# Two Mamba layers with states of eight channels on the partitions instead of one state of 128 channels at a time

## The chip, the cores and the metric

The kernel runs on one core of one Trainium2 chip. The metric is device time in microseconds of one execution of the whole program. The engines named here are PE (TensorE, the matrix array), DVE (VectorE), ACT (ScalarE), POOL (GpSimd) and SP (which issues most of the transfers). Each has a queue of instructions that it takes in order; they meet at semaphores. SBUF is the on-chip memory of 128 partitions, PSUM the smaller memory that PE writes to, in 8 banks of 512 f32 per partition.

## What is computed

The reference is a network of four layers on an image batch `x` of shape (4, 56, 56, 128), all in f32. Layer 0 is a windowed attention, layer 1 a pair of Mamba blocks, layer 2 an additive attention and an expert layer, layer 3 an attention and a mixture of experts. Each result is added to `x`. Only layer 1 and the group norm in front of layers 0 and 1 are touched. Cut to what matters, layer 1 is:

```python
h = gn(x).reshape(b * n, t, d)            # 4*56 sequences of 56 steps, d = 128
for l in range(2):
    u, res = split(h @ in_w[l])           # 256 inner channels each
    u = silu(causal_depthwise_conv(u, conv_w[l], 4 taps) + conv_b[l])
    dt, Bm, Cm = split(u @ x_proj_w[l], [8, 24])    # 8 + 16 + 16
    delta = softplus(dt @ dt_proj_w[l] + dt_proj_b[l])
    A = -exp(A_log[l])                    # (256, 16)
    # per sequence, for each channel d and each state n, s starts at 0:
    #   s[t,d,n] = exp(delta[t,d] * A[d,n]) * s[t-1,d,n] + delta[t,d] * u[t,d] * Bm[t,n]
    #   y[t,d]   = sum_n s[t,d,n] * Cm[t,n]
    h = ((y + u * D[l]) * silu(res)) @ out_proj_w[l]
x = x + h
```

There are 256 x 16 = 4096 independent recurrences over time for each sequence.

## The kernel before

Everything stays on the chip between the layers. `X[b]` holds image b as 28 tiles of 112 tokens (two image rows each). Layer 1 works on chunks of CH = 448 tokens, which are SEQ = 8 whole sequences of HW = 56 steps. There are NCH = 7 chunks an image, 4 images and 2 Mamba blocks, so 56 pairs of a chunk and a block; I call one such pair a step. For an image the order is chunks 0 to 3 of block 0, the same of block 1, then chunks 4 to 6 likewise (`order` in `layer1`).

For a step the 256 inner channels lie on the partitions in NHALF = 2 halves of 128, time along the free dimension. `mamba_pre` prepares a step: the input projection on PE, the copy into a padded tile `up` (L480), the causal convolution as one `tensor_scalar` and three `scalar_tensor_tensor` per half on DVE (L483, L488), Silu on ACT, the projection `dbl` to dt, B and C (L500), delta with a softplus built from Abs, Exp and Ln on ACT and four operations on POOL (L515 to L523), and du = delta * u on DVE (L525).

`mamba_scan` then loops over the DS = 16 states. For state n, PE broadcasts the row of B and the row of C to all partitions by a matmul with a column of the identity (L541), ACT makes dA = exp(A * delta) with A as a scale per partition (L549), DVE makes dBu = B * du (L553), runs the recurrence over 2 x 448 elements as one scan (L555), and multiplies by C (L559); PE adds the product into y with an identity matmul (L561). The decay tiles `dA` have a zero at the first step of every sequence, so that one scan restarts at each. In the middle of the loop (n = 8) `midway` issues the preparation of the next step. At the end DVE forms yg = (u * D + y) * silu(res) (L566, L569) and PE projects it.

The tile framework decides the order in each engine's queue when the program is built, from the program's order and its own estimates, and gives buffers from pools of a fixed number (`bufs`). So a line of the loop can stand in a queue a little before or behind its place in the text, but not past what its pool allows. All loads of a layer's weights are issued by SP at the layer's start, when the previous layer's memory is free.

`group_norm` transposes an image by PE into PSUM, copies it (alternately DVE and ACT), takes statistics of the copy on DVE (L143), combines them over groups of four channels by a small matmul, and normalises in place (L161). It is called once per image in layer 0 and in layer 1.

Of the kernel before, what the change touches and what calls it, by code (L numbers as in the profile page):

```python
# [35 lines left out]
DBL = DR + 2 * DS  # L36

# [16 lines left out]
def host_constants():  # L54
# [7 lines left out]
    for d in range(KR):  # L62
# [5 lines left out]
    place[p, QW - JG + p // AH] = 1.0  # L68
    return {
        "k_toep": toep.reshape(1 + KR, HW * HW),  # L70
# [6 lines left out]
class Hybrid:  # L77
# [57 lines left out]
    def group_norm(self, b, pool, psum, tag, group):  # L135

        nc = self.nc
        xn = self.t(pool, [P, S], "xnT")
        st = self.t(pool, [P, NCH, nc.vector.BN_STATS_DIM], "gn_st")
        for c in range(NCH):  # L140
            ch = xn[:, c * CH : (c + 1) * CH]
            self.transposed_chunk(psum, tag, self.X[b], c, ch)
            nc.vector.bn_stats(st[:, c, :], ch)  # L143
# [15 lines left out]
        for c in range(NCH):  # L159
            ch = xn[:, c * CH : (c + 1) * CH]  # L160
            nc.vector.tensor_scalar(ch, ch, mean, r, op0=ALU.subtract, op1=ALU.mult)  # L161
# [122 lines left out]
    def layer0(self):  # L284
        nc, a, tc = self.nc, self.a, self.tc
        with ExitStack() as ctx:
# [24 lines left out]
            for b in range(B):  # L311
                xn = self.group_norm(b, big, ps_m, "m", group)
# [74 lines left out]

    def layer1(self):
        nc, a, tc = self.nc, self.a, self.tc
        with ExitStack() as ctx:  # L390
            wp = ctx.enter_context(tc.tile_pool(name="l1_w", bufs=1))
            w = {}
            group = self.load(wp, [P, P], "group1", a["k_group"])
            w["in"] = self.load(
                wp, [P, NL, 2 * DI], "in_w", a["L1_conv_in_proj_w"].rearrange("l p f -> p l f")
            )
            by_channel = lambda n, r: a[n].rearrange(r, p=P)
            w["xw"] = self.load(
                wp, [P, NL, NHALF, DBL], "xw", by_channel("L1_conv_x_proj_w", "l (h p) k -> p l h k")
            )  # L400
            w["dtw"] = self.load(
                wp, [DR, NL, DI], "dtw", a["L1_conv_dt_proj_w"].rearrange("l r d -> r l d")
            )
            w["ow"] = self.load(
                wp, [P, NL, NHALF, C], "ow", by_channel("L1_conv_out_proj_w", "l (h p) m -> p l h m")
            )
            w["A"] = self.load(
                wp, [P, NL, NHALF, DS], "A", by_channel("L1_conv_A_log", "l (h p) n -> p l h n")
            )
            nc.scalar.activation(w["A"], w["A"], AF.Exp)  # L410
            nc.vector.tensor_scalar(w["A"], w["A"], -1.0, None, op0=ALU.mult)
            w["cw"] = self.load(
                wp, [P, NL, NHALF, DC], "cw", by_channel("L1_conv_conv_w", "l (h p) o k -> p l h (o k)")
            )
            with nc.allow_non_contiguous_dma(reason="vectors, by partition"):
                for k, n in (("cb", "conv_b"), ("dtb", "dt_proj_b"), ("D", "D_param")):
                    w[k] = self.load(
                        wp, [P, NL, NHALF], k, by_channel("L1_conv_" + n, "l (h p) -> p l h")
                    )

            w["dA"] = []
            for i in range(3):
                dA = self.t(wp, [P, NHALF, SEQ, HW], f"dA{i}")
                nc.vector.memset(dA, 0.0)
                w["dA"].append(dA)
            self.n_dA = 0

# [3 lines left out]
            ps_b = ctx.enter_context(tc.tile_pool(name="l1_b", bufs=2, space=PSUM))  # L431
            ps_y = ctx.enter_context(tc.tile_pool(name="l1_y", bufs=1, space=PSUM))
            for b in range(B):
                xn = self.group_norm(b, big, ps_m, "m", group)


                h = {c: xn[:, c * CH : (c + 1) * CH] for c in range(NCH)}
# [4 lines left out]
                for i, (c, l) in enumerate(order):  # L442
# [5 lines left out]
                    yg = self.mamba_scan(l, w, pre.pop((c, l)), sm, ps_b, ps_y, prepare_next)  # L448
                    if l < NL - 1:
                        po = self.t(ps_m, [P, 512], "m")  # L450
                        for f in range(NHALF):
                            nc.tensor.matmul(
                                po[:, :CH], w["ow"][:, l, f, :], yg[:, f],
                                start=(f == 0), stop=(f == NHALF - 1),
                            )
                        h[c] = self.t(sm, [P, CH], "h", bufs=5)
                        nc.scalar.copy(h[c], po[:, :CH])
                        continue
# [10 lines left out]
    def mamba_pre(self, l, h, w, sm, ps_m):  # L469

        nc = self.nc
        seqs = lambda ap: ap.rearrange("p (s t) -> p s t", t=HW)
        us = self.t(sm, [P, NHALF, CH], "us")
        sres = self.t(sm, [P, NHALF, CH], "sres")
        for f in range(NHALF):
            ps = self.t(ps_m, [P, 512], "m")
# [4 lines left out]
            u = us[:, f]  # L481
            cw = w["cw"][:, l, f, :]
            nc.vector.tensor_scalar(  # L483
                seqs(u), up[:, :, DC - 1 :], cw[:, DC - 1 : DC], w["cb"][:, l, f : f + 1],
# [488 lines left out]
```

## Time and profile before

| what | value |
|---|---|
| median of 3 runs | 11,997.65 us (11,997.62 to 12,001.13) |
| profiled execution | 12,008.86 us, span 12,007.1 us |
| mean granted clock of PE | 0.896 |
| PE busy | 10,754.4 us, 90% |
| DVE busy | 5,358.3 us, 45% |
| ACT busy | 6,301.1 us, 52% |
| POOL busy | 668.6 us, 6% |

The profile describes one execution. A group line names the kernel line, the engine, the operation, the tiles and shapes and the count, then after the bar the busy time of the group in us and the mean duration of one in ns, then the idle time of the engine just before these instructions and what ended it. An f32 matmul appears as two records. The matmuls' ends are modelled, so the start-to-start time says more than the duration. The granted clock is the share of full speed that PE was given; a window line gives it for a stretch. A line of a stretch gives the window, its length, and for each engine the busy time and the number of instructions.

The layers follow one another in time: layer 0 to about 1045 us, layer 1 to about 5750, the additive attention to about 8900, the rest to the end. In the row of 40 slices each slice is 300 us.

### The profile page before, as it was taken

The page shows a single profiled execution, that of the slowest core. Times are in us where ns is not written, and L with a number is a line of the kernel's source. Part 1 is how long each engine was busy: PE and PEld are TensorE (multiplying, and loading weights), DVE is VectorE, ACT ScalarE, POOL GpSimd, SP SyncE. Part 2 cuts the span into 40 slices and gives each one's busy share as a digit, 9 for nine tenths or more (in the row PEclk, how much of TensorE's full clock was granted, in tenths as well). Part 3 has the DMA queues.
Part 4 walks back from the last instruction along what each step waited for, and adds up shares of the span by engine and source line. Part 5 has one row for each costly group of instructions (what it writes and reads, how often), then busy time and mean ns, then how long its engine had stood idle before and what let it go on. Part 6 is the DMA issues. An engine that isn't in the chain of part 4 may idle for free.

```text
span 12007.1 us, 105563 instructions
## 1 busy us (share of the span) xinstructions
PE 10754.4 (90%) x41247; PEld 4699.9 (39%) x41247; DVE 5358.3 (45%) x7960; ACT 6301.1 (52%) x10749; POOL 668.6 (6%) x494
## 2 busy tenths in 40 slices
PE   7888888888988888888899999999999979998988
PEld 3443333333333333333333333333333358655655
DVE  3446898888988888888300000000000031123033
ACT  2223443334434343443799899899899911322322
POOL 0000111111111111111000000000000000000000
PEclk8887888888888888888999999999999956999999
DMA  1000000000000000000000000000000012000000
GB/s 36 1 1 4 0 0 0 0 0 0 0 0 0 0 0 0 0 0 0 1 1 1 1 1 1 1 1 1 1 1 1 1 50 65 1 6 6 1 6 6
DMA packets 90323, 59.06 MB, mean 5 GB/s; under 512 B 21012, under 2 KB 81244, under 8 KB 89756
## 3 DMA queue, kind: packets, MB, share of 16 engines
q1 hardware_dynamic: 89821, 52.30, 1.6%
q8 instruction: 324, 5.31, 0.2%
q14 instruction: 178, 1.45, 0.0%
HBM read 45.21 MB, written 7.07 MB: 4 GB/s over the span
## 4 chain that ended last, share of the span: by engine, by line
PE 67%; DVE 16%; issue 7%; ACT 6%; POOL 4%; SPq 0%; DMA 0%; ACTq 0%; POOLq 0%; DVEq 0%
PE s L651 24%; PE y L561 8%; PE o L851 7%; PE s L844 5%; DVE hs L555 4%; PE o L660 4%; PE C L541 3%; DVE hs L559 3%; PE B L541 2%; ACT e L656 2%; DVE dBu L553 2%; PE d L369 2%; PE o L369 2%; DVE us L488 2%; POOL sp_e L521 1%
## 5 line engine op out<-in xcount | busy, mean ns | idle before, releaser
L646 ACT ACTIVATE th<-fT,g 128x448 f32<-128x448 f32 (+3 forms) x6272 | 3328.9, 622 | 17.5 <-DVE g L627 17.5
L651 PE MATMUL s<-th,place 128*32 128x448 f32 (+4 forms) x12544 | 3183.1, 515 | 7.0 <-ACT th L646 7.0
L549 ACT ACTIVATE dA<-delta,A 128x440 f32<-128x440 f32 x1792 | 1092.8, 654 | 2296.7 <-DVE hs L555 2289.3
L671 DVE TENSOR_SCALAR den<-o 112x1 f32<-112x1 f32 x224 | 31.8, 152 | 4961.7 <-PE o L660 3644.1
L561 PE MATMUL y<-hs,ident 128*128 128x448 f32 x3584 | 1795.7, 639 | 427.6 <-DVE hs L559 424.1
L555 DVE TENSOR_TENSOR_SCAN hs<-dA,dBu 128x896 f32<-128x896 f32 x896 | 1797.2, 2024 | 0.6
L651 PEld LDWEIGHTS s<-th,place 128*32 128x32 f32 (+1 forms) x12544 | 786.7, 106 | 2131.9 <-ACT th L646 2032.5
L561 PEld LDWEIGHTS y<-hs,ident 128*128 128x128 f32 x3584 | 730.3, 220 | 1474.0 <-DVE hs L559 814.2
L541 PE MATMUL B<-dbl,ident 40*128 40x448 f32 x1792 | 900.4, 607 | 186.0 <-DVE dBu L553 185.5
L559 DVE TENSOR_TENSOR hs<-C,hs 128x896 f32<-128x896 f32 x896 | 947.4, 1077 | 49.5 <-PE C L541 48.2
L849 ACT ACTIVATE e<-s,shift 112x448 f32<-112x448 f32 x784 | 496.3, 634 | 886.4 <-PE s L844 839.0
L553 DVE TENSOR_TENSOR dBu<-B,du 128x896 f32<-128x896 f32 x896 | 943.0, 1074 | 0.0
L541 PE MATMUL C<-dbl,ident 40*128 40x448 f32 x1792 | 880.3, 593 | 0.0
L851 PEld LDWEIGHTS o<-xa,e 112*112 112x112 f32 x6272 | 711.1, 176 | 297.5 <-ACT e L849 295.6
L851 PE MATMUL o<-xa,e 112*112 112x129 f32 x6272 | 789.3, 279 | 13.5 <-ACT e L849 0.9
L844 PE MATMUL s<-xT 128*112 128x448 f32 x1568 | 654.6, 539 | 0.0
L541 PEld LDWEIGHTS B<-dbl,ident 40*128 40x128 f32 x1792 | 340.5, 202 | 648.1 <-DVE dBu L553 341.6
L660 PE MATMUL o<-xa,e 112*112 112x129 f32 x3248 | 492.3, 288 | 106.2 <-ACT e L656 98.5
L660 PEld LDWEIGHTS o<-xa,e 112*112 112x112 f32 x3248 | 384.5, 176 | 447.2 <-ACT e L656 402.5
L357 ACT ACTIVATE e<-s 112x896 f32<-112x896 f32 (+1 forms) x272 | 206.4, 801 | 602.0 <-PE s L352 434.9
L541 PEld LDWEIGHTS C<-dbl,ident 40*128 40x128 f32 x1792 | 299.6, 192 | 536.9 <-issue 491.8
L361 DVE TENSOR_TENSOR e<-e,e_inner 112x560 f32<-112x560 f32 (+5 forms) x416 | 238.2, 612 | 358.5 <-ACT e L357 357.3
(218 smaller groups left out, 7666.3 us busy)
## 6 DMA issues: line engine op xcount, KB each, us to landing
w<-in_L_ffn_weight SPq DMA_DIRECT2D x16, 1024.0 KB
w<-in_L_ffn_weight SPq DMA_DIRECT2D x64, 256.0 KB
X<-in_x SPq DMA_DIRECT2D x8, 784.0 KB
out<-X SPq DMA_DIRECT2D x8, 784.0 KB
e_edge<-dtab SPq DMA_DIRECT2D x42, 49.0 KB
e_inner<-dtab SPq DMA_DIRECT2D x14, 49.0 KB
dtab<-tab SPq DMA_DIRECT2D x1, 637.0 KB
in_w<-in_L_conv_in_proj_w SPq DMA_DIRECT2D x1, 512.0 KB
```

What stands on the lines that cost most here:

```text
L541: nc.tensor.matmul(ps[:, :CH], self.ident[0:DBL, at : at + 1].to_broadcast([DBL, P]), dbl, start=True, stop=True,)
L549: nc.scalar.activation(dA[:, f, :, 1:], seqs(delta[:, f])[:, :, 1:], AF.Exp, scale=w["A"][:, l, f, n : n + 1])
L553: nc.vector.tensor_mul(dBu, bc[0], du)
L555: nc.vector.tensor_tensor_scan(hs.rearrange("p f c -> p (f c)"), dA.rearrange("p f s t -> p (f s t)"), dBu.rearrange("p f c -> p (f c)"), ...
L559: nc.vector.tensor_mul(hs, bc[1], hs)
L561: nc.tensor.matmul(py[f][:, :CH], self.ident, hs[:, f], start=(n == 0), stop=(n == DS - 1))
L646: nc.scalar.activation(th[:, lo:], fT[:, c * CH + lo : (c + 1) * CH], AF.Tanh, bias=g[:, at : at + 1])
L651: nc.tensor.matmul(ps[QW * blk : QW * blk + rows, lo:CH], place[:, off : off + rows], th[:, lo:], start=(q == 0), stop=(n + 1 == NG or q = ...
L660: nc.tensor.matmul(po[s][:TP, : C + 1], e[:, s * TP : (s + 1) * TP], xa[:, J, :], start=(J == 0), stop=(J == TC * c + s),)
L844: nc.tensor.matmul(ps[:TP, :CH], xT[:, t * TP : (t + 1) * TP], xT[:, c * CH : (c + 1) * CH], start=True, stop=True,)
L849: nc.scalar.activation(e, ps[:TP, :CH], AF.Exp, bias=shift)
L851: nc.tensor.matmul(po[s][:TP, : C + 1], e[:, s * TP : (s + 1) * TP], xa[:, t, :], start=(t == 0), stop=(t == NT - 1),)
```

## The change

Layer 1 is rearranged so that 8 channels x 16 states lie on the 128 partitions.

- The loop over 16 states becomes a loop over 32 groups of eight channels, taken in pairs: 16 iterations a step, each with two groups `k` that sit in different quarters of 32 partitions. Per group, PE expands delta of 8 channels to 128 partitions with the factor -A folded into the selection matrix (`A`, L606: 32 rows by 128 columns, so that the two groups' matmuls use different row tiles of the array), ACT takes Exp of both groups in place in PSUM (L609), PE expands du likewise (`u`, L613), DVE multiplies it with B (L617) and scans 448 elements with the decay read from PSUM (L618).
- The product with C moves to POOL, one instruction over both groups (L621).
- The sum over the 16 states is a matmul with a 0/1 matrix of 128 x 32 (`sum`, L623), into 32 partitions of y, so that the two groups use different column tiles. u * D enters y as a matmul with a diagonal matrix (L597), and the gating is one product per half (L627).
- B and C come replicated from a matmul with a weight of 128 columns (L556), two per chunk and half.
- The convolution is folded into the input projection: four weights, one per tap, and four accumulating matmuls over shifted views of h (L539), so h and the normalised x carry three zeros before each sequence. The bias enters at the Silu.
- delta comes straight from u by a weight that is the product of the two small projections (L567), formed once. The restart of the scans comes from setting delta to 1e30 at each sequence's first step (L586), so that the decay is exp(-large) = 0. du is made on POOL (L582).
- The weights that this needs are formed once on DVE and PE in `layer1_weights`.
- `group_norm` takes its statistics from PSUM, not from the copy, and can leave room for the zeros.

The core of the diff:

```diff
-        nc.vector.tensor_mul(du, delta, us)
-        return us, sres, dbl, delta, du
+        nc.gpsimd.tensor_mul(du, delta, us)
+        first = delta.rearrange("p f (s t) -> p f s t", t=HW)[:, :, :, 0:1]
+        for f in range(NHALF):
+            nc.gpsimd.memset(first[:, f], LONG)
+        return us, sres, bc, delta, du
...
-        py = [self.t(ps_y, [P, 512], f"y{f}") for f in range(NHALF)]
-        for n in range(DS):
-            if n == DS // 2:
-                midway()
-            bc = []
-            for tag, at in (("B", DR + n), ("C", DR + DS + n)):
-                ps = self.t(ps_b, [P, 512], tag)
-                nc.tensor.matmul(
-                    ps[:, :CH], self.ident[0:DBL, at : at + 1].to_broadcast([DBL, P]), dbl,
-                    start=True, stop=True,
-                )
...
-            for f in range(NHALF):
-                nc.scalar.activation(
-                    dA[:, f, :, 1:], seqs(delta[:, f])[:, :, 1:], AF.Exp, scale=w["A"][:, l, f, n : n + 1]
-                )
-            nc.vector.tensor_mul(dBu, bc[0], du)
-            nc.vector.tensor_tensor_scan(
...
-            nc.vector.tensor_mul(hs, bc[1], hs)
...
         for f in range(NHALF):
+            py = self.t(ps_m, [P, 512], "m")
+            nc.tensor.matmul(py[:, :CH], w["Dd"][:, l, f, :], us[:, f], start=True, stop=False)
+            for r0 in range(0, P // HD, 2):
+                for q in range(QG):
+                    if (f, r0, q) == (0, 2, 2):
+                        midway()
+                    pa = self.t(ps_a, [P, 2, 512], "a")
+                    hs = self.t(sm, [P, 2, CH], "hs", bufs=3)
+                    for k in range(2):
+                        own = rows(r0 + k)
+                        nc.tensor.matmul(
+                            pa[:, k, :CH], w["A"][own, l, f, q, :], delta[own, f], start=True, stop=True
+                        )
+                    nc.scalar.activation(pa[:, :, :CH], pa[:, :, :CH], AF.Exp)
+                    for k in range(2):
+                        own = rows(r0 + k)
+                        pu = self.t(ps_u, [P, 512], "u")
+                        nc.tensor.matmul(
+                            pu[:, :CH], w["pick"][own, q, :], du[own, f], start=True, stop=True
+                        )
+                        dBu = self.t(sm, [P, CH], "dBu", bufs=3)
+                        nc.vector.tensor_mul(dBu, pu[:, :CH], bc[:, 0])
+                        nc.vector.tensor_tensor_scan(
+                            hs[:, k], pa[:, k, :CH], dBu, 0.0, op0=ALU.mult, op1=ALU.add
+                        )
+                    nc.gpsimd.tensor_mul(hs, hs, bc[:, 1:2].to_broadcast([P, 2, CH]))
+                    for k in range(2):
+                        nc.tensor.matmul(
+                            py[rows(r0 + k), :CH], w["sum"][:, q, :], hs[:, k],
+                            start=False, stop=(q == QG - 1),
+                        )
+            nc.vector.tensor_mul(yg[:, f], py[:, :CH], sres[:, f])
```

In `mamba_pre` the convolution and the small projections:

```diff
-            nc.tensor.matmul(ps[:, :CH], w["in"][:, l, f * P : (f + 1) * P], h, start=True, stop=True)
-            up = self.t(sm, [P, SEQ, HW + DC - 1], f"up{f}")
-            nc.gpsimd.memset(up[:, :, 0 : DC - 1], 0.0)
-            nc.scalar.copy(up[:, :, DC - 1 :], seqs(ps[:, :CH]))
...
+            for k in range(DC):
+                nc.tensor.matmul(
+                    seqs(ps[:, :CH]), w["in"][:, l, k, own], h[:, :, k : k + HW],
+                    start=(k == 0), stop=(k == DC - 1),
+                )
+            nc.scalar.activation(us[:, f], ps[:, :CH], AF.Silu, bias=w["cb"][:, l, f : f + 1])
...
+        for i in range(2):
+            ps = self.t(ps_m, [P, 512], "m")
+            for f in range(NHALF):
+                nc.tensor.matmul(
+                    ps[:, :CH], w["bc"][:, l, i, f, :], us[:, f], start=(f == 0), stop=(f == NHALF - 1)
+                )
+            nc.scalar.copy(bc[:, i], ps[:, :CH])
...
+            for g in range(NHALF):
+                nc.tensor.matmul(
+                    ps[:, :CH], w["dt"][:, l, g, f * P : (f + 1) * P], us[:, g],
+                    start=(g == 0), stop=(g == NHALF - 1),
+                )
```

The pools of layer 1 in PSUM are `ps_m` (2 banks: y, and every product of the preparation), `ps_a` (2 x 2 banks) and `ps_u` (2 banks); before, they were `ps_m` (2), `ps_b` (2 each for B and C) and `ps_y` (2).

More of the change, by code (lines that the diff above doesn't have):

```diff
@@ L159, in group_norm @@
         for c in range(NCH):
[L160 to L161 removed]
+            nc.vector.tensor_scalar(chunk(c), chunk(c), mean, r, op0=ALU.subtract, op1=ALU.mult)
         return xn
@@ L391, in layer1 @@
             wp = ctx.enter_context(tc.tile_pool(name="l1_w", bufs=1))
[L392 to L395, printed above, removed]
-            )
-            by_channel = lambda n, r: a[n].rearrange(r, p=P)
-            w["xw"] = self.load(
-                wp, [P, NL, NHALF, DBL], "xw", by_channel("L1_conv_x_proj_w", "l (h p) k -> p l h k")
-            )
[L401 to L426, printed above, removed]
+            w = self.layer1_weights(wp)
             big = ctx.enter_context(tc.tile_pool(name="l1_big", bufs=2))
```

168 lines of the change are left out of this document (110 added, 58 removed).

## Prediction

> **What bounds the kernel now.** I read the page first (busy times, slices, costliest groups), then stretches of the second stage, then groups by shape. From the page:
> ```profile
> PE 10754.4 (90%) x41247; PEld 4699.9 (39%) x41247; DVE 5358.3 (45%) x7960; ACT 6301.1 (52%) x10749; POOL 668.6 (6%) x494
> DVE  3446898888988888888300000000000031123033
> PEclk8887888888888888888999999999999956999999
> L555 DVE TENSOR_TENSOR_SCAN hs<-dA,dBu 128x896 f32<-128x896 f32 x896 | 1797.2, 2024 | 0.6
> L553 DVE TENSOR_TENSOR dBu<-B,du 128x896 f32<-128x896 f32 x896 | 943.0, 1074 | 0.0
> L559 DVE TENSOR_TENSOR hs<-C,hs 128x896 f32<-128x896 f32 x896 | 947.4, 1077 | 49.5 <-PE C L541 48.2
> ```
> The shares mix stages. The changed stage is where the DVE digits are 8 and 9, 1093 to 5748 us; scan and products there (L553, L555) have next to no idle time before them: VectorE is the bound. One step (one chunk, one layer; 56 in all) runs from one gating (L566) to the next, 2514.45 to 2595.80. Busy times of PE, PEld, DVE, ACT, POOL, then the granted clock:
> ```profile
> 100.00:1040.00 940.00, 801.59 (x5488) 377.71 (x5485) 417.79 (x668) 233.56 (x317) 25.88 (x21) 0.80 0.00 1
> 2514.45:2595.80 81.35, 71.60 (x153) 26.83 (x152) 73.37 (x63) 32.91 (x49) 11.25 (x6) 0.90 0.00 0
> 449.18:452.59 3.41, 2.06 (x26) 1.24 (x26) 1.31 (x3) 1.88 (x3) 0.00 (x0) 1.00 0.00 0
> 452.59:456.00 3.41, 3.41 (x27) 1.62 (x24) 1.10 (x3) 0.00 (x0) 0.00 (x0) 0.50 0.02 5
> ```
> A step is 81.35 us, DVE 73.37 of it; 56 x 81.35 = 4556 of the stage's 4655. Rows 3 and 4 show the clock: a stretch in which PE was busy 2.06 of 3.41 us is followed by one at half clock. The other prices, from groups by shape and matmuls in order of time:
> ```profile
> L357 ACT ACTIVATE e<-s 112x896 f32<-112x896 f32 x224 | 196.4, 915 | 526.1 <-PE s L352 434.9 <-issue 84.9 <-ACT e L357 6.3
> L377 DVE TENSOR_TENSOR oT<-o,r 128x448 f32<-128x448 f32 x28 | 17.2, 613 | 0.1
> L523 POOL TENSOR_TENSOR delta<-delta,sp_ln 128x896 f32<-128x896 f32 x56 | 116.9, 2087 | 4.4
> 601.34 0.73 PE L352 MATMUL s<-qT,kT 32*112 32x280 f32 x4 [0.98 <-ACT e L357]
> 2586.25 1.01 PE L541 MATMUL C<-dbl,ident 40*128 40x448 f32 x2
> 2587.10 0.91 PE L541 MATMUL B<-dbl,ident 40*128 40x448 f32 x2
> 2587.95 1.77 PE L561 MATMUL y<-hs,ident 128*128 128x448 f32 x4
> ```
> An f32 matmul leaves two records; start to start, one of 448 columns takes 0.85 us (C to B to y). L352's four records are two matmuls in different row tiles, done in the time of one, so a pair of row tiles costs about 0.9, and so do two column tiles.
>
> **The change by engine, per step.** DVE loses 16 x (1.07 + 2.02 + 1.08) = 66.7, the convolution 2 x (0.50 + 3 x 0.68) = 5.1, du 1.09 and 1.2 of the gating. It gains 32 products at 0.61 (L377) and 32 scans, each half of L555 and a share of fixed cost, 1.08: 54.1. About 57 remain: 16 us less. PE has 3 pairs in each of 16 iterations (A, u, sum; about 41 us) and some 20 single matmuls for the next chunk (convolution 8, gate 2, B and C 4, delta 4, D 2; 16 us). POOL gains 16 products at 2.07 and du. The memsets it gains (two of 8 columns on delta, one on h; L479's 0.12 each) replace two of `up`. ACT's table loads (1.28) rise from 4.5 to 10, since four Silu now stand between Exp; its busy time is 16 x 0.92 + 7 + 13 = 35 in 105, and only the two loads counted below lie on the path. No engine is full in 81 us, so the order decides.
>
> **The order of the built program.** PE takes its queue in order. Sum(i) needs POOL's product of iteration i, which needs both scans of i. The queue repeats two forms: "A(i) u0(i) sum(i-1) u1(i)" in 7 of 16 iterations (split), else "A(i) u0 u1 sum(i-1)". Behind each sum stand A(i+1) and, when split, u1(i), so VectorE's next product waits for POOL, and the scan behind it too.
> Let E(i) be the end of the second scan. Split: POOL 2.07 + 0.07 handover, sum 0.85, u1 0.8, drain and handover 0.2, then product and scan 1.6: E(i) = E(i-1) + 5.6. An unsplit one after it is bound by DVE, 3.2. Unsplit behind unsplit: E(i+1) = E(i-1) + 2.14 + 0.85 + 0.9 + 0.75 + 0.2 + 3.2 = E(i-1) + 8.0, 4.0 each. The sequence is 13 to 15 unsplit, 0 and 1 split, 2 unsplit, 3 split, 4 unsplit, 5 split: 3.2 + 4.8 + 3.2 + 6.1 (with 0.5 of the gating product) + 5.6 + 3.2 + 5.6 + 3.2 + 5.6 = 40.5 for 9 iterations.
> The preparation falls into iterations 6 to 12:
> - 5 to 6: POOL 2.14, sum 0.85, A 0.9, u0 0.75, four convolution matmuls 3.0 in the queue before u1, u1 1.0, product and scan 1.6 = 10.2. 6 to 7: 5.6.
> - 7 to 12: POOL 2.14, sum 0.85, u1 0.75, half of A 0.75, eight matmuls (B, C, delta) 6.0, drain 0.2: 10.7. ACT: Abs 0.63, load 1.28, Exp 0.95, the iteration's Exp 0.95, load 1.28, Ln 0.95: 6.0. POOL: softplus add 2.07, add-subtract 3.2, product 9, three more (du with them), and only then product 10: 6 x 2.07 + 3.2 = 15.6. Then sum 0.85, A 0.9, u0 0.95, DVE 1.6, u1 and the rest 1.6: 5.9. Total 38.2.
> Together 54; the step is 54.0 + 40.5 = 94.5 at full clock, against 81.35. Before, the chain through POOL showed once a step, as 6.35 us of idle DVE ahead of du, because no product of the scan stood in POOL's queue; moving du to POOL removes that wait and its 1.09, and product 10 and sum(10) are late next.
> PE work on that path is 20 us in iterations 6 to 12 and 10 in the others. At half clock the step is 94.5 + 30 = 124.5. A pair of iterations keeps PE busy 5.7 of 8.8 us, about the share (2.06 of 3.41) after which the clock fell; at half clock PE is nearly always busy, after which it came back. The first stage, which alternates so (PE busy 0.85 of it), has a mean of 0.80, that is 0.4 of the time at half clock; I take that: 1 / (0.6/94.5 + 0.4/124.5) = 105 us a step. Its bounds are 94.5 (always full) and 124.5 (always half).
> The Trainium skill, "TensorE: Matmul & The Clock Gate", section "Why this matters for your kernels", asks for no PE-idle gaps over about 3 us to avoid a drop; by that the clock stays full here and the time would be 12,730 (an estimate); the row at 449 us shows a drop with 2.06 of 3.41 us busy, and I follow the row.
> "TensorEngine Tiling (Array Packing)", section "Key Properties", says that changing the tiling mode drains TensorE, which speaks against alternating row and column tiles; a drain of 0.16 us (a record's 0.54 less 0.38 of streaming) twice an iteration would be 5 us a step, some 290 in all (estimate); no row here has that switch without a wait, and the sum leaves it out.
>
> **Small parts.** Weights: 13 loads in place of 11 on SP (0.4 to 0.8 each to issue), a 1 MB broadcast, and some 30 DVE instructions at 0.2 to 0.6 stand before the first group norm's statistics or beside them, where three clears (2.7) stood: 0 to 20 once; I take 15, nearest to the DVE sum. Group norm reads statistics from PSUM: 0.61 (L377, PSUM) against 0.62, 56 times: nothing, at most 4 either way. The first preparation of a batch runs uncovered before and after (33 us before: 1060.7 to 1093.8); 5 to 10 more, four times. Against that, the last step of each batch has none to carry: 54 less 7 iterations at 4.3, that is 24, against some 13 (convolution, delta and du on DVE 7.6, the wait 6.35), four times. These cancel within 60, and I count them as nothing.
>
> **Sum.** 56 x (105 - 81.35) = +1324 on the profiled execution's 12,008.9 (span 12,007.1): 13,333. The median before, 11,997.65, stands 11 lower: 13,320.
> Prices that no row has: the scan of 448 with one input in PSUM is at least half of L555, 1.01, and at most 1.08 + 0.18 (a 448 tensor_scalar took 0.68 from PSUM, L516, and 0.50 from SBUF, L483); I take 1.08, nearest to L555; the upper end is 32 x 0.18 = 5.8 a step, 325 in all. Exp in place in PSUM over 2 x 448: L357 has 0.92 for the same shape read from PSUM, and two of L549 make 1.3; the path holds it once a step (iteration 9; elsewhere it ends 0.3 before the scan needs it), so 0.4 a step, 22 in all; I take 0.95. POOL's product with a broadcast factor: L523 has 2.07 for 896, and the add with a broadcast in the first stage 1.27 for 512, which is 2.2 for 896; the upper end adds 8 x 0.15, 67 in all.
>
> **Rivals.**
> - Full clock throughout: 94.5 a step, 12,008.9 + 56 x 13.15 - 11 = 12,730. For it: 2507 to 2547 us ran at 0.99; against it: PE was 96% busy there.
> - Row tiles not side by side, or half clock nearly always: pairs of A and u at 1.7 in place of 0.9, 14 a step on top of 105 (A on 16 paths at 0.8, u partly), or 124.5 straight: 13,320 + 784 = 14,100 to 14,410. L352's row is against the first, but with 112 columns, not 128.
> - Faster: POOL's product is much quicker than L523. POOL holds 8 x 2.14 + 15.6 = 33 of the 94.5; at full clock the break-even is a saving of 13.15, all of POOL at 0.6 of its rows, the product at about 1.25 us instead of 2.07. At 1.1 the step is 79 and the time 11,870; with POOL wholly out of the way (DVE 57 and the 8 that it idles now) 11,080. For it: POOL's busy spans are rough; against it: L520, L522 and L523 lie at 2.07 to 2.4, and a sum(i) released by DVE alone isn't in the program.
> - No change: 105 would have to fall to 81; nothing else does that.
>
> **How the numbers follow.** Chances: the forecast 0.52 (own range 12,950 to 13,800), full clock 0.22, the slow rival 0.17, faster 0.08, same 0.01. The range leaves out the faster case, the lower edge of the full-clock case and the upper of the slow one: 12,500 to 14,300. A difference under 0.2% can't be told from none here.
>
> **What would show it.** After: DVE busy near 57 us a step with its largest idle put down to PE u; PE's largest wait for POOL hs (L621 of the changed kernel); iterations of 3.2 and 5.6 in turn; a clock near 0.80 in this stage; one stall of some 15 us a step behind POOL's softplus. I am wrong if L621 is near 1.1 us, if the clock digits stay 9, or if the row tiles start 0.85 apart.

## The result, and the profile of the changed kernel

The changed kernel takes 14,229.17 us (median of 4 runs, 14,225.5 to 14,234.95), the kernel before 11,997.64 beside it: a ratio of 1.186, with a 95% interval of 1.184 to 1.188. The forecast was 13,320 with a range of 12,500 to 14,300. Sign and range hold, but the time lies 429 us above the top of the likeliest case's own range (12,950 to 13,800) and inside the slow rival's (14,100 to 14,410). So the forecast case is not the one that came. Of the slow rival's two conditions, half clock for most of the time is the one that came; its other, row tiles that do not run side by side, did not. That the range holds is in part luck: it reaches 14,300 only because it takes in some of that rival.

The profile page of the changed kernel, in the same rows as before: busy time of PE, two rows of slices, and the groups of the scan's iteration.

```profile
PE 12578.3 (88%) x46187; PEld 4988.1 (35%) x46187; DVE 4432.1 (31%) x8336; ACT 6291.4 (44%) x10061; POOL 2585.3 (18%) x1478
DVE  4444444444444444444444300000000003130332
PEclk8786666666666666666666799999999996699999
L621 POOL TENSOR_TENSOR hs<-hs,bc 128x896 f32<-128x896 f32 x896 | 1858.0, 2074 | 3761.4 <-DVE hs L618 3568.2
L613 PE MATMUL u<-du,pick 32*128 32x448 f32 x3584 | 2328.0, 852 | 75.7 <-DVE dBu L617 75.7
L617 DVE TENSOR_TENSOR dBu<-u,bc 128x448 f32<-128x448 f32 x1792 | 1098.5, 613 | 2801.6 <-PE u L613 2581.1
L618 DVE TENSOR_TENSOR_SCAN hs<-a,dBu 128x448 f32<-128x448 f32 x1792 | 1946.7, 1089 | 279.3 <-ACT a L609 185.7
```

VectorE's digits fell from 8 and 9 to 4: it is no longer the bound. The new thing is the clock's row: sixes throughout the second stage, whose last gating now stands at 7965 us in place of 5744. L617 idles 2801.6 us in all, nearly all of it put down to PE's u.

Stretches of the changed kernel: 4000 us of the stage, one step, and four neighbouring stretches of 3.41 us (busy times of PE, PEld, DVE, ACT, POOL, then the granted clock).

```profile
1300.00:5300.00 4000.00, 3375.26 (x7914) 1099.51 (x7914) 1843.24 (x2288) 1086.77 (x1176) 1458.62 (x772) 0.62 0.00 0
3073.70:3196.60 122.90, 105.06 (x238) 33.01 (x240) 55.79 (x69) 34.29 (x37) 44.61 (x23) 0.61 0.00 0
...
3098.18:3101.60 3.42, 3.42 (x9) 1.17 (x6) 0.83 (x1) 0.07 (x1) 2.08 (x1) 0.50 0.00 0
3101.60:3105.01 3.41, 3.41 (x7) 0.69 (x6) 1.72 (x2) 2.11 (x2) 0.00 (x0) 0.50 0.00 0
3105.01:3108.42 3.41, 3.41 (x5) 1.17 (x4) 1.71 (x2) 0.00 (x0) 0.12 (x1) 0.50 0.00 0
3108.42:3111.84 3.42, 3.42 (x6) 1.35 (x4) 0.00 (x0) 0.00 (x0) 1.96 (x1) 0.50 0.00 0
```

A step takes 122.9 us here (median of all steps 121.9; 81.3 before). The last four rows matter most: PE is busy for the whole of each, and the clock stays at half. The prediction had counted on the opposite, that a busy stretch brings the clock back.

Longest waits of the changed kernel, 1200 to 7900 us (total us, times, longest):

```profile
POOL hs L621 <- DVE hs L618: 3471.0, 696, 11.4
DVE dBu L617 <- PE u L613: 2509.1, 812, 19.3
...
PEld m L623 <- POOL hs L621: 1446.0, 498, 7.4
```

The ring VectorE, POOL, PE, VectorE that the prediction describes stands in these three rows. PE's matmuls in order of time, changed kernel:

```profile
3097.93 1.71 PE L623 MATMUL m<-hs,sum 128*32 128x448 f32 x4 [1.51 <-POOL hs L621]
3099.57 1.86 PE L606 MATMUL a<-delta,A_pick 32*128 32x448 f32 x4
3101.22 1.70 PE L613 MATMUL u<-du,pick 32*128 32x448 f32 x2
3102.85 1.71 PE L623 MATMUL m<-hs,sum 128*32 128x448 f32 x4
3104.49 1.86 PE L613 MATMUL u<-du,pick 32*128 32x448 f32 x2
3106.27 6.01 PE L539 MATMUL m<-xnT,in_w 128*128 128x448 f32 x8
```

Each line is two matmuls side by side (x4) or one (x2). At half clock each takes 1.63 to 1.78 start to start, and PE has no gap after the first sum: PE itself becomes the bound. The split form puts u0 and u1 on both sides of the sum, so they cannot run side by side.

### The profile page after: what moved, and what is told of

The parts are those of the page before. It is cut to its first block, busy times and chain, and to the rows that moved or that the text cites. A ratio compares the mean times of both kernels' runs of the same rounds, so it can differ in the third digit from the quotient of the medians.

```text
span 14223.5 us, 117225 instructions
## 1 busy us (share of the span) xinstructions
PE 12578.3 (88%) x46187; PEld 4988.1 (35%) x46187; DVE 4432.1 (31%) x8336; ACT 6291.4 (44%) x10061; POOL 2585.3 (18%) x1478
## 4 chain that ended last, share of the span: by engine, by line
PE 73%; POOL 10%; DVE 9%; ACT 5%; issue 2%; SPq 0%; DMA 0%; POOLq 0%; DVEq 0%; ACTq 0%
PE s L709 20%; PE m L623 9%; PE u L613 8%; POOL hs L621 7%; PE o L909 6%; PE a L606 5%; PE s L902 4%; DVE hs L618 3%; PE m L539 3%; PE o L718 3%; DVE dBu L617 2%; PE m L556 2%; ACT e L714 2%; PE d L386 1%; PE o L386 1%
## 5 line engine op out<-in xcount | busy, mean ns | idle before, releaser
L621 POOL TENSOR_TENSOR hs<-hs,bc 128x896 f32<-128x896 f32 x896 | 1858.0, 2074 | 3761.4 <-DVE hs L618 3568.2
L613 PE MATMUL u<-du,pick 32*128 32x448 f32 x3584 | 2328.0, 852 | 75.7 <-DVE dBu L617 75.7
L609 ACT ACTIVATE a<-a 128x896 f32<-128x896 f32 x896 | 807.7, 902 | 3555.5 <-PE a L606 2360.0
L623 PE MATMUL m<-hs,sum 128*32 128x448 f32 x3584 | 1393.4, 874 | 924.8 <-POOL hs L621 892.3
L618 DVE TENSOR_TENSOR_SCAN hs<-a,dBu 128x448 f32<-128x448 f32 x1792 | 1946.7, 1089 | 279.3 <-ACT a L609 185.7
L617 DVE TENSOR_TENSOR dBu<-u,bc 128x448 f32<-128x448 f32 x1792 | 1098.5, 613 | 2801.6 <-PE u L613 2581.1
L606 PE MATMUL a<-delta,A_pick 32*128 32x448 f32 x3584 | 1870.2, 893 | 33.8 <-POOL delta L586 29.3
L613 PEld LDWEIGHTS u<-du,pick 32*128 32x128 f32 x3584 | 818.3, 279 | 1248.1 <-issue 979.6
L606 PEld LDWEIGHTS a<-delta,A_pick 32*128 32x128 f32 x3584 | 564.7, 273 | 880.5 <-issue 776.5
L623 PEld LDWEIGHTS m<-hs,sum 128*32 128x32 f32 x3584 | 160.3, 133 | 1949.0 <-POOL hs L621 1487.2
```

What stands on the lines that cost most here:

```text
L606: nc.tensor.matmul(pa[:, k, :CH], w["A"][own, l, f, q, :], delta[own, f], start=True, stop=True)
L609: nc.scalar.activation(pa[:, :, :CH], pa[:, :, :CH], AF.Exp)
L613: nc.tensor.matmul(pu[:, :CH], w["pick"][own, q, :], du[own, f], start=True, stop=True)
L617: nc.vector.tensor_mul(dBu, pu[:, :CH], bc[:, 0])
L618: nc.vector.tensor_tensor_scan(hs[:, k], pa[:, k, :CH], dBu, 0.0, op0=ALU.mult, op1=ALU.add)
L621: nc.gpsimd.tensor_mul(hs, hs, bc[:, 1:2].to_broadcast([P, 2, CH]))
```

## The experiments

All kernels compute the whole result. The table's times are of one run each, but for before, changed, e10 and e13; the kernel before, run beside them on three chips, ranged from 11,983 to 12,027, so a difference of that size between two rows means nothing. Step is the median length; clock and PE busy are of 1300 to 5300 us.

| kernel | time, us | step, us | clock | PE busy |
|---|---|---|---|---|
| before | 11,998 | 81.3 | 0.86 | 85% |
| changed | 14,229 | 121.9 | 0.62 | 84% |
| A and u in 64 rows (e12) | 13,607 | 110.6 | 0.81 | 76% |
| u in 128 rows (e9) | 13,297 | 105.0 | 0.90 | 82% |
| A and u in 128 rows (e2) | 13,347 | 105.9 | 0.94 | 83% |
| softplus on VectorE (e4) | 14,014 | 119.4 | 0.61 | 89% |
| product on VectorE (e1) | 12,925 | 96.5 | 0.70 | 93% |
| sums late (e3) | 12,433 | 91.7 | 0.80 | 90% |
| sums late, u in 128 rows (e6) | 12,226 | 86.5 | 0.93 | 92% |
| e6, half of each product on VectorE (e8) | 12,294 | 87.1 | 0.95 | 92% |
| e6, four products on VectorE (e11) | 12,001 | 81.9 | 0.97 | 94% |
| e11, convolution unfolded (e10) | 12,029 | 81.9 | 0.94 | 93% |
| e11, but A and u in paired tiles of 64 rows (e13) | 11,929 | 80.5 | 0.94 | 92% |
| before, convolution folded (e7) | 12,232 | 85.3 | 0.81 | 93% |

Two theories stood against each other. The order theory: the ring through POOL makes PE wait, the clock falls because of the waits, and a queue without them brings both back. The tile theory: matmuls that use few rows of the array count for little with whatever grants the clock, so that it stays low however busy PE is.

### The product on VectorE (e1)

```diff
-                    nc.gpsimd.tensor_mul(hs, hs, bc[:, 1:2].to_broadcast([P, 2, CH]))
+                    nc.vector.tensor_mul(hs, hs, bc[:, 1:2].to_broadcast([P, 2, CH]))
```

> The product with C back on DVE, all else as changed. After the change a step takes 122 us at a mean clock of 0.62. Order theory (PE's queue stands behind POOL's product, and the low clock follows from those waits): no instruction of the loop waits for POOL any more, DVE has 57 + 17 = 74 us a step and is the bound again with some 10 us lost around the preparation, 85 us a step, about 12,200 us, clock over 0.8. Tile theory (matmuls that use 32 rows or 32 columns of the array do not count as activity, so the clock stays low whatever waits, and PE at half clock is the bound): three pairs at 1.65 us in 16 iterations are 79, twenty matmuls at 1.5 are 30, so 109 us a step, about 13,550 us, clock still near 0.6.

Measured: 12,925, 96.5 us a step, stage clock 0.70. Neither expectation holds alone. Taking POOL out of the ring is worth 1,304 us (the framework ordered PE's queue anew for it, which has an unknown share in this). But with PE busy 93% of the stage, the clock is still only 0.70, which waits cannot explain.

### More rows in the tiles, same queue (e2, e9, e12)

e2 gives A and u weights over all 128 rows, zero outside a tile's own 32; the group norm's buffers go from two sets to one to make room. e9 does that for u alone. e12 pairs tiles 64 rows apart and widens each to 64 rows, so that pairs still run side by side:

```diff
 e9
-                            pu[:, :CH], w["pick"][own, q, :], du[own, f], start=True, stop=True
+                            pu[:, :CH], w["pick"][:, (r0 + k) * QG + q, :], du[:, f], start=True, stop=True
 e12
-                        own = rows(r0 + k)
+                        own = slice(k * P // 2, (k + 1) * P // 2)
...
-                            py[rows(r0 + k), :CH], w["sum"][:, q, :], hs[:, k],
+                            py[rows(r0 + 2 * k), :CH], w["sum"][:, q, :], hs[:, k],
```

In all three, PE's queue holds the scan's and the preparation's matmuls in exactly the changed kernel's order.

> The selection matmuls A and u over all 128 rows with zero weights in the rows of other groups, in place of row tiles of 32: the same results, the same queue orders, pairs no longer side by side. (The pool of the normalised image has one buffer in place of two, for room.) At full clock this adds 0.75 us to each A pair and each u pair. Tile theory: the array counts as busy, the clock of the stage rises from 0.62 to over 0.85, and the step is 94 + 14 = 108 at full clock, at most 115: about 13,500 us, faster than the changed kernel. Order theory: the waits are as before, the clock stays near 0.62 or rises only as PE fills, and a step gains 16 x 1.5 / 0.62 = 39: 160 us, about 16,400 us.

> The changed kernel with only the matmuls of u over all 128 rows; the sums, and A in row tiles, are as they were. It has the same queue orders as the changed kernel (121.9 us a step at clock 0.62) and more PE work. If narrow row tiles keep the clock down: clock 0.72 to 0.85, a step of 108 to 116, time 13,450 to 13,900, between the changed kernel and the one with A and u over 128 rows (105.9 at 0.94). If the clock only follows PE's waits: 0.62, time 14,230 to 14,600.

> The changed kernel with one thing different: the two tiles of 32 rows that make a pair (matmuls of A and u) are taken 64 rows apart and widened to 64 rows each, with zero weights for the 32 rows that are not theirs. PE's queue has the same matmuls in the same order, pairs stay pairs, VectorE, ACT and POOL have the same work. If the share of the rows in use sets the granted clock: 0.85 to 0.95 in place of 0.62, a step of 96 to 106 (the prediction's order at full clock gave 94.5; with u's split pair still apart), time 12,800 to 13,360. If the clock follows PE's waits alone, or the number of matmuls: 0.62 and 14,200 as before. If tiles of 64 rows do not run side by side: the clock up, the step near the 105.9 of the kernel with 128 rows, 13,350.

Measured: 13,347, 13,297 and 13,607; clock 0.94, 0.90 and 0.81 where the changed kernel has 0.62. e2 came 150 us under the 13,500 of the tile theory. e9 missed its range too, on the good side: 13,450 to 13,900 at a clock of 0.72 to 0.85 was expected. e12 missed its range (12,800 to 13,360, clock 0.85 or more) by 250 us, but its direction cannot be had from the order theory: beside the rows, only the quarters that make a pair differ, and with them the columns that the sums use; in e9 the sums are the changed kernel's. e2 and e9 even add work to PE, since u's pairs no longer overlap, and still gain 880 and 930 us.

The stage in e9, e12 and e2, then e12 in stretches of 3.41 us, to be held against the four rows of the changed kernel above:

```profile
1300.00:5300.00 4000.00, 3272.83 (x9193) 1076.55 (x9194) 2151.09 (x2646) 1271.35 (x1373) 1680.83 (x886) 0.90 0.00 0
```

```profile
1300.00:5300.00 4000.00, 3036.94 (x8736) 1033.30 (x8736) 2018.70 (x2511) 1207.10 (x1305) 1590.09 (x838) 0.81 0.00 0
```

```profile
1300.00:5300.00 4000.00, 3306.99 (x9095) 1336.93 (x9095) 2126.96 (x2620) 1254.06 (x1355) 1670.76 (x883) 0.94 0.00 0
```

```profile
3101.95:3105.37 3.42, 3.42 (x10) 1.18 (x8) 0.52 (x1) 0.90 (x1) 2.07 (x1) 0.50 0.00 0
3105.37:3108.78 3.41, 3.41 (x14) 1.11 (x12) 3.04 (x4) 0.90 (x1) 0.00 (x0) 1.00 0.00 0
...
3112.19:3115.61 3.42, 3.42 (x8) 1.34 (x7) 0.25 (x1) 0.00 (x0) 2.07 (x1) 0.50 0.00 0
3115.61:3119.02 3.41, 3.41 (x14) 1.12 (x12) 2.14 (x3) 0.90 (x1) 0.00 (x0) 1.00 0.00 0
```

One full stretch at half clock, then full clock: here the rule that the prediction leaned on works. Over 1300 to 5300 us I counted, from the trace's clock records, how many stretches with PE busy throughout at half clock were followed by full clock: 92 of 512 in the changed kernel (18%), 207 of 273 in e12 (76%), 106 of 138 in e9 (77%), 76 of 76 in e2. For the same queue the share rises with the rows in use.

### The sums two iterations late (e3)

```diff
-                    for k in range(2):
-                        nc.tensor.matmul(
-                            py[rows(r0 + k), :CH], w["sum"][:, q, :], hs[:, k],
-                            start=False, stop=(q == QG - 1),
-                        )
+                    late.append((py, hs, r0, q, f))
+                    if len(late) > 2:
+                        add_up(mm.ins)
```

The two matmuls of a sum now belong to the iteration two before, and stand behind u1 of the running one in PE's queue; `hs` has five buffers in place of three.

> Each sum stands two iterations behind its product in PE's queue (behind the u of iteration i + 2, ahead of A of i + 3), with five buffers for the states in place of three; same instructions otherwise. Order theory: PE no longer waits for POOL in the loop, E(i+1) is at most E(i-2) + 8.0, 2.7 an iteration, under DVE's 3.2; DVE at 57 a step plus the stall behind POOL's softplus, 9 to 12: 68 us a step, about 11,250 us, PE over 80% busy and the clock over 0.85. Tile theory: PE at half clock is the bound, 79 + 30 = 109 us a step, about 13,550 us, clock near 0.6 with PE nearly always busy.

Measured: 12,433, 91.7 us a step, clock 0.80: between the two expectations. The order is worth 1,796 us, more than any other single edit, with what follows from it: a higher clock, and u's pairs side by side more often. Yet the step stays 10 above the 81.3 of the kernel before. PE in this kernel, in order of time:

```profile
3119.33 1.71 PE L603 MATMUL m<-hs,sum 128*32 128x448 f32 x4
3120.97 1.86 PE L621 MATMUL a<-delta,A_pick 32*128 32x448 f32 x4
3122.63 1.70 PE L628 MATMUL u<-du,pick 32*128 32x448 f32 x4
3124.26 1.71 PE L603 MATMUL m<-hs,sum 128*32 128x448 f32 x4
3125.90 1.86 PE L621 MATMUL a<-delta,A_pick 32*128 32x448 f32 x4
3127.55 1.70 PE L628 MATMUL u<-du,pick 32*128 32x448 f32 x4
3129.19 1.71 PE L603 MATMUL m<-hs,sum 128*32 128x448 f32 x4
3130.82 4.65 PE L539 MATMUL m<-xnT,in_w 128*128 128x448 f32 x8
3135.41 1.02 PE L621 MATMUL a<-delta,A_pick 32*128 32x448 f32 x4
```

Here no wait is left, all pairs are side by side, PE is busy without a gap for 11 us, and the clock stays at half (1.64 start to start) until the convolution's matmuls over all 128 rows come; after those A takes 0.95 again. These nine lines are what the tile theory expects.

### Late sums and u in 128 rows (e6), then the product shared out (e8, e11)

e6 joins e3 and e9; PE's queue is that of e3. e8 and e11 are e6 with:

```diff
 e8
-                    nc.gpsimd.tensor_mul(hs, hs, bc[:, 1:2].to_broadcast([P, 2, CH]))
+                    nc.gpsimd.tensor_mul(hs[:, 0], hs[:, 0], bc[:, 1])
+                    nc.vector.tensor_mul(hs[:, 1], hs[:, 1], bc[:, 1])
 e11
-                    nc.gpsimd.tensor_mul(hs, hs, bc[:, 1:2].to_broadcast([P, 2, CH]))
+                    eng = nc.vector if (f, r0) == (1, 0) else nc.gpsimd
+                    eng.tensor_mul(hs, hs, bc[:, 1:2].to_broadcast([P, 2, CH]))
```

> The kernel with the sums two iterations late, and in addition the matmuls of u over all 128 rows (weights zero outside the tile's own 32 rows); A stays in row tiles. With the sums late alone a step took 91.7 us at a granted clock of 0.80. If narrow row tiles are what keeps the clock down: clock 0.88 to 0.95 in the stage, a step of 82 to 86, time 11,900 to 12,150, although u0 and u1 can no more run side by side. If the clock only follows PE's waits: the clock stays at 0.80, the steps get longer where u0 and u1 ran side by side (up to 9 x 0.75 us a step), 12,430 to 12,800.

> As the kernel with late sums and u over 128 rows, but of each product with C the first half (448) on POOL and the second on VectorE. VectorE 57 + 16 x 0.61 = 67 us a step, POOL 16 x 1.05 + 15.6 = 32, PE 16 x 3.25 + 20 = 72 at full clock. If the order and the clock are the whole cost: a step of 76 to 80, time 11,690 to 11,920, faster than before. If row tiles of A are enough to keep the clock near 0.8: 86 to 90 a step, 12,250 to 12,480.

> Late sums, u over 128 rows, the products of iterations 8 to 11 on VectorE, the convolution folded. The step with POOL's products in all iterations was 86.5 us, with 7 us in which PE waited for POOL behind softplus. If that wait goes: 79 to 82 us, 11,800 to 11,990. If PE's work is the bound and the wait only lets the queue catch up, no change: 85 to 87, 12,150 to 12,240. Against the kernel with the convolution unfolded as well, the difference is what the fold costs or brings here: PE's six matmuls, 5.1 us a step or 286 in all, if PE is the bound.

Measured: e6 12,226 (clock 0.93 as the tile theory said, the step 0.5 above its range and the time 76); e8 12,294, a miss on both sides, since the clock is 0.95 and the step still 87.1; e11 12,001, 11 above its range. The clock effect adds to the order's: 207 us more on top of e3. PE in e6:

```profile
3112.32 1.02 PE L629 MATMUL a<-delta,A_pick 32*128 32x448 f32 x4
3113.27 1.77 PE L635 MATMUL u<-du,pick 128*128 128x448 f32 x4
3114.97 0.94 PE L611 MATMUL m<-hs,sum 128*32 128x448 f32 x4
3115.84 1.02 PE L629 MATMUL a<-delta,A_pick 32*128 32x448 f32 x4
```

An iteration is 0.95 + 1.70 + 0.87 = 3.52 us of PE with no gap: 56 us in sixteen, and with some 20 for the next chunk 76 at full clock. So PE is the engine nearest to being the bound of these kernels (92% busy in e6, 94% in e11). That it alone sets the step is not shown: e10 and e13 below take work off it and gain little or nothing. e11, which takes away the stall behind softplus by giving VectorE the four products that stood there, comes to 81.9 at a clock of 0.97. In e8 VectorE's products cost more than the 0.61 assumed (see the last section).

### Softplus off POOL (e4)

```diff
-        nc.gpsimd.tensor_add(ln, ln, e)
+        nc.vector.tensor_add(ln, ln, e)
...
-        nc.gpsimd.tensor_mul(du, delta, us)
+        nc.vector.tensor_mul(du, delta, us)
```

> The four operations of softplus and du go to DVE; POOL keeps only the product and the memsets. Both theories: products 9 and 10 no longer stand behind 3.2 + 4 x 2.07 = 11.5 us of POOL's queue, DVE gains 5 x 1.0 = 5 us on the same chain, so a step loses 6 to 7 us: 115 us, about 13,850 us. If DVE operations with two inputs in SBUF are held up by POOL's products, as the scan and the convolution of the kernel before were (2.5 to 2.9 us in place of 0.7 to 2.0), up to 2 us for each of the five is given back: 125 us, 14,400 us. The clock stays near 0.62 in either case.

Measured: 14,014, between the two. With the sums where they were, taking the five instructions out of POOL's queue is worth 215 us, 2.5 us in the median step. PE's queue is not quite the changed kernel's (the output projection of the step's first half stands five iterations earlier). The clock stayed at 0.61, and PE at half clock (89% busy) was there to take the stall's place; this last part is argued from the rows and not tested by itself.

### The convolution alone (e7, e10)

e7 is the kernel before with the convolution folded, and with it the changed group norm, which leaves room for the zeros; e10 is e11 with the convolution unfolded again, in the old code.

```diff
 e7
-            nc.tensor.matmul(ps[:, :CH], w["in"][:, l, f * P : (f + 1) * P], h, start=True, stop=True)
...
-            for k in range(DC - 1):
-                nc.vector.scalar_tensor_tensor(
+            for k in range(DC):
+                nc.tensor.matmul(
+                    seqs(ps[:, :CH]), w["in"][:, l, k, own], h[:, :, k : k + HW],
```

> The kernel before with the convolution folded into the matmuls as the one change. VectorE loses 2 x (0.50 + 3 x 0.68) = 5.1 us a step, of which it was the bound: if all of it counts, 81.35 - 5.1 = 76.2 us a step and 11,710; if PE's six matmuls more (5.1 us) take their place on the path, no change, 11,980 to 12,010. In either case this part does not explain a time above 12,000.

> Late sums, u over 128 rows, the products of iterations 8 to 11 on VectorE (those behind softplus in POOL's queue), and the convolution back on VectorE as in the kernel before. PE then has 16 x 3.53 = 56.5 us for the iterations and 16 matmuls for the next chunk, 13.6: 70; VectorE 57 + 5 + 5 = 67. If PE's queue is what bounds the kernel with late sums and u over 128 rows (86.5 us a step): 74 to 79 us, time 11,580 to 11,870, faster than before. If the convolution on VectorE delays the scans by as much as PE gains: 80 to 84, 11,920 to 12,150.

e7: 12,232, slower than before by 226 us, where I had expected 11,710 or no change, and had written that this part could not explain a time above 12,000. It can, by itself. VectorE's first product of the iteration (1300 to 5300 us), kernel before, then e7:

```profile
L553 DVE TENSOR_TENSOR dBu<-B,du 128x896 f32<-128x896 f32 x767 | 806.7, 1074 | 0.0
```

```profile
L563 DVE TENSOR_TENSOR dBu<-B,du 128x896 f32<-128x896 f32 x728 | 769.6, 1079 | 404.4 <-PE B L551 404.0
```

VectorE lost 5.1 us of work a step and gained a wait of 8.6 (404.0 in 4000 us, at 85.3 a step). PE in e7 shows it:

```profile
3062.19 3.17 PE L496 MATMUL m<-xnT,in_w 128*128 128x448 f32 x8
3065.20 1.91 PE L503 MATMUL m<-xnT,res_w 128*128 128x448 f32 x4
3067.04 1.70 PE L510 MATMUL m<-us,xw 128*40 128x448 f32 x4
3068.67 1.01 PE L551 MATMUL B<-dbl,ident 40*128 40x448 f32 x2
```

Four convolution matmuls and four more of the preparation stand in one block of 6.5 us ahead of the broadcast of B, on which VectorE then waits, up to 10.2 us. The stage's clock fell from 0.86 to 0.81 as well; how much of the 226 us is the clock's was not tested.

e10: 12,029.21 in 10 runs, a ratio to before of 1.0021 (1.0011 to 1.003), where 11,580 to 11,870 was expected if PE's queue is the bound. It falls into the other case, that the convolution delays VectorE's scans by as much as PE gains (80 to 84 a step, 11,920 to 12,150). Taking six matmuls off PE brought nothing against e11 (28 us the other way), while VectorE's busy time rose from 61 to 66 us a step (2978.1 and 3224.0 us in 4000). One thing to be seen in e10's trace is that A's two matmuls no longer stand together:

```profile
3121.06 1.02 PE L541 MATMUL m<-h,in_w 128*128 128x448 f32 x2
3122.01 1.01 PE L635 MATMUL a<-delta,A_pick 32*128 32x448 f32 x2
3122.95 1.02 PE L541 MATMUL m<-h,in_w 128*128 128x448 f32 x2
3123.90 1.01 PE L635 MATMUL a<-delta,A_pick 32*128 32x448 f32 x2
```

A pair that should take 0.95 takes twice that. How much of the missing 5.1 us this makes, and how much VectorE's added work, was not tested.

### Tiles of 64 rows, late sums, four products on VectorE (e13)

> Tiles of 64 rows, the sums two iterations late, and the products of iterations 8 to 11 on VectorE, the convolution folded. An iteration then needs 2.77 us of PE (A 0.95, u 0.95, sum 0.87), a step 44 + 20 = 64 of PE and 57 + 5 = 62 of VectorE. If rows and order were the two costs of the change: clock over 0.9, a step of 68 to 76, time 11,260 to 11,700, faster than before. If the clock stays near the 0.80 of the late sums with 32 rows: 84 to 88, 12,050 to 12,380.

Measured: 11,928.99 in 4 runs (11,926.77 to 11,931.73), a ratio to before of 0.9931 (0.9915 to 0.9948): faster than both kernels, by 0.7% and by 16% (11,929 of 14,229). The clock is 0.94 as expected; the step, 80.5, is not the 68 to 76 of the sum, and the time lies between the two expectations. PE in e13:

```profile
3113.21 0.94 PE L606 MATMUL m<-hs,sum 128*32 128x448 f32 x4
3114.08 1.02 PE L624 MATMUL a<-delta,A_pick 64*128 64x448 f32 x4
3116.47 1.02 PE L631 MATMUL u<-du,pick 64*128 64x448 f32 x2 [1.36 <-DVE dBu L635]
3118.20 1.02 PE L631 MATMUL u<-du,pick 64*128 64x448 f32 x2 [0.72 <-DVE dBu L635]
```

u0 and u1 pair up only when both of u's two PSUM buffers are free. Where VectorE has just released one, they run one after the other, each behind a product, and PE and VectorE wait for each other in turn. More buffers for u would need a bank that A or the running sums hold now; that was not tried. VectorE's four products of a step also take 2.7 us longer in all than they would alone (last section).

## Why the prediction was right and wrong

**VectorE's 57 us and the prices: right.** 55.79 us in the step shown. (The losses and gains that the prediction lists would leave 53.4 of the 73.37, not 57, since the durations of neighbouring instructions overlap in the busy time; 57 is what the new durations add up to.) The product took 613 ns (0.61 predicted), the scan 1089 (1.08), Exp 902 (0.95), POOL's product 2074 (2.07). None of the unknown prices decided anything.

**The ring through POOL: right in kind, short in size.** Where an iteration ran wholly at full clock, the split form took 5.97 (5.6 predicted), the one after it 3.38 in e12 (3.2), and the iteration of the convolution 10.88 in e12 (10.2). From the end of iteration 7 to that of 12 the prediction had 38.2; on average it took 45.6 in the changed kernel and 41.6 in e9, at clock 0.90. The last step of each batch, which has no preparation, is 23.7 us shorter (98.2 against 121.9); the prediction had 24. The late sums bear out the ring: with the same instructions, the sums elsewhere and two more buffers for `hs`, they win 1,796 us, though a part of that is the clock, which rose from 0.62 to 0.80.

**The clock: the step that failed.** The prediction took 0.80, "0.4 of the time at half clock", from the first stage, and gave as reason that at half clock PE is nearly always busy, "after which it came back". The stage has 0.62, that is 0.76 of the time at half clock. With that share the prediction's own formula gives 1 / (0.24/94.5 + 0.76/124.5) = 115.7 us in place of 105: 10.7 of the 16.9 that the step was short (121.9), some 600 us over 56 steps. The other 6.2, some 350, are put down to the ring's prices above. (Together 950; the times differ by 909.) An estimate supports the split: with both bounds 6.1 higher, 100.6 and 130.6, the formula gives 121.9 for the changed kernel's clock, and some 110 and 105 for e12's and e9's, which have its order and took 110.6 and 105.0. The reason failed because a busy PE was not enough: 82% of the fully busy stretches at half clock were followed by another one. What the runs put in its place: with the same queue, the clock rises with the rows that A's and u's tiles use (0.62, 0.81, 0.94 for 32, 64 and 128).

**The row that was read for the clock.** The first stage has matmuls of 32 rows too, among others of 128 (L352 in the prediction), and its mean of 0.80 was a mixture like any. Carrying it over assumed that only the busy share matters. The Trainium skill, "TensorE: Matmul & The Clock Gate", section "What's actually happening", says that the clock returns after one busy window of about 3.4 us; the runs agree for matmuls over all rows (76 of 76 in e2) and not for tiles of 32 rows (92 of 512). The same page's rule on idle gaps (section "Why this matters for your kernels"), which the prediction set aside, would have been further off: 12,730 by the prediction's estimate.

**Row tiles side by side: right, and no rescue.** Pairs start together, and the drain between tiling modes does not show: in e6's rows above, two u take 1.70, the sum 0.87 and the pair of A 0.95, against 0.85 for a single matmul, so at most 0.1 us a change. At half clock a pair costs 1.64, and split u cannot pair.

**The stall behind softplus: there, and worth less than priced.** 15.6 us of POOL were on the path by the sum; taking them out of POOL's queue brought 2.5 a step in the changed kernel (e4). With the order and the clock mended, where less stood ready to take its place, giving four products to VectorE brought 4.6 a step (86.5 to 81.9; the clock rose from 0.93 to 0.97 with it).

**Small parts.** Of the 2,216 us between the two profiled spans, all but some 43 lie between the first and the last gating of the stage. The prediction did see the convolution's block in PE's queue, in iteration 5 to 6; that this block outweighs the 5.1 us which VectorE sheds, even in the kernel before (226 us), it did not say.

## What to carry to other kernels

Matmuls packed as narrow row tiles may run side by side and still leave the clock at half; compare the clock of a version with zero-filled wider tiles before counting on their price, and put the halves of a pair 64 rows apart where the layout allows it. Ask of each matmul that waits for a slow engine what stands behind it in PE's queue: moving it two iterations back was the largest single gain here. Work that leaves the bounding engine is not a gain if it lands as one block ahead of what that engine waits for.

## What the runs showed of the hardware

- The granted clock depends on more than PE's busy time. With an identical queue it was 0.62 for tiles of 32 rows and 0.94 for 128 rows of which 96 have zero weights, while PE was busy 84% and 83%. What exactly is counted stays open: with late sums, u in 128 rows raised the share of stretches that regain full clock from 78 of 325 to 60 of 95, not to all, and in the kernel before, whose broadcasts use 40 rows, it is 121 of 194.
- VectorE's product of two SBUF operands is slowed by most of POOL's work beside it. The form of 896 elements in e13 (min, median and max in ns):

```profile
L640 DVE TENSOR_TENSOR hs<-hs,bc x224: 1081/1092/2742, 1147.2 to 5651.3; 128x896 f32<-128x896 f32 x112
```

Of its 224 instances, the 120 that no POOL work overlaps took 1.09 us, the 104 with POOL at work for over 90% of their time 2.52 (median). In e8, the form of 448 took 0.63 alone and 1.32 so beside POOL. But not every POOL instruction does it: 47 of e8's products lay wholly beside the `tensor_scalar` of softplus on POOL, which reads SBUF, and took 0.63 (POOL's spans are rough). The changed kernel's product and scan, which take one operand from PSUM, kept 613 and 1089 ns although POOL's product ran beside them. This agrees with the Trainium skill, "SBUF — State Buffer", section "Who interferes with whom", which says that a VectorE instruction with two SBUF inputs contends with a GpSimd instruction that reads SBUF, but for the `tensor_scalar`, where the measurement does not bear it out. In e8 VectorE's half of the product took 0.78 on average, 2.5 us a step more than alone; that may be a part of why e8 brought nothing.
